# Lots of the two routers, place of the weight reads and of the residual reads in a fused two-layer kernel

## The chip, the cores and the metric

The kernel runs on one core of a Trainium2 chip. The metric is the device time of one execution in microseconds (us). Three executions of the kernel before are shown with their median, and one further execution was recorded by the hardware profiler. A core has five engines that run at the same time and wait for each other by semaphores: PE multiplies matrices, DVE, ACT and POOL work on tiles element by element, SP issues most of the DMA transfers. Each engine does its instructions in the order in which the program lists them.

## The reference, cut to what matters

There are 4096 tokens (64 sequences of 64) of 256 numbers. Four residual layers follow one another; the change lies in the last one, which has two mixtures of experts in a row, and in the end of the third, during which parts of the last are already worked.

```python
x = x + attn0(scan0(x, cond))
x = x + ffn0(cond2(x, cond))
x = x + mamba(rnn(x, cond))                    # x_mid: the kernel's name for this sum
x = x + ffn1(cond2_1(x, cond))

def cond2_1(x, t):                             # first mixture
    shared = sum(silu(x @ s_w1[e].T) * (x @ s_w3[e].T) @ s_w2[e].T for e in range(2)) / 2
    s = sigmoid(concat(x, t) @ W_router.T)     # 8 experts
    top = top_k(s + router_bias, 2)
    gates = s[top] / (sum(s[top]) + 1e-9)      # 0.5 each where the sum is not over 1e-9
    routed = sum(gates[e] * gelu(x @ r_w1[e].T) @ r_w2[e].T for e in top)
    return (shared + routed) / 4

def ffn1(x):                                   # second mixture
    score, top = top_k(x @ Wg.T, 2)            # 8 experts
    return sum(score[e] * (silu(x @ W1[e].T) * (x @ W2[e].T)) @ W3[e].T for e in top)
```

## The kernel before

Tokens are worked in 8 chunks of 512. Mamba (L684 to L952) takes 32 steps for each chunk: a step multiplies the input by B on POOL (hb, L864), exponentiates on ACT (dA, L871), scans on DVE (L903, two of them), multiplies by C on DVE (L905) and turns the product into a sum on PE (yp, L919). POOL's product is made two steps ahead. Between the steps a written-out order advances other work piece by piece: `urgent` and `pieces` are Mamba's own next parts (head, gates, finish, project), and `others` is the work beside it, at BESIDE (56) pieces for 32 steps. When `project` (L832) has written a chunk's x_mid (L846) it works off what is left of `others` and starts `beside` of the class Mixture (L1384) for that chunk. So the pieces of chunk c run during the period of chunk c + 1, and the last chunk's stay for later.

The pieces of a chunk are: the first router's scores, `choose` where a half of the tokens has its scores (L1401, after chunk 3: 16 tiles of 128 tokens at once), the `send` of a chunk of the first half (L1429), and `shared`, the shared expert of the chunk (L1446). `choose` makes the masks of the two best experts, counts with a scan and two products on PE how many tokens each expert has got so far, and from that the row of each token in a buffer in memory, in which every expert has a region (`Routing.choose`, L1045). `send` reads the chunk of x_mid, transposes it on PE (L1441), copies it into rows of 260 numbers on ACT (L1442), adds tags (L1436) and writes these with 8 indirect DMAs issued by POOL (L1100). Chunks 0 and 1 are sent during the periods of chunks 5 and 6 and chunks 2 and 3 during that of chunk 7. The pool of this work has one buffer of a kind.

After Mamba `mixtures` (L1541) runs. `rest` (L1484) reads the last chunk, makes its scores, chooses for the second half of the tokens (16 tiles), and sends chunks 4 to 7 while it works off the last chunk's shared expert: the up-products L1459, the product on POOL L1467, and the down-products L1475. `tiles` (L1123) makes a table of 39 tiles of 256 rows of the regions (L1131 to L1172). `Experts.run` (L1204) works them in order. `load` of a tile (L1209) reads two numbers of the table into registers of SP, asks for the weights of the tile's expert and then for its rows (`read`, L1105), which must wait until every send has landed. `turn` transposes the rows (L1224), `up` and `down` are the expert's products, and `give` (L1112) writes the result's rows by an indirect DMA of POOL. In the second experts (`Swiglu`) the up-products are L1335 and the weights of a tile (L1318 to L1323) have 2.16 MB.

Between the two lies the loop over chunks: `combine` (L1500) reads the shared expert's rows and the two experts' rows of each token (L1120) and adds them on DVE (L1507), and `Gate.chunk` (L1520) transposes the sum, makes the second router's scores, chooses for the chunk's 4 tiles and sends the chunk. At last a stage over the 8 chunks reads the second experts' rows and x_mid (L1563), adds them on PE (L1569) and DVE (L1578) and writes the output (L1579).

Memory on the core comes from pools that are opened and closed like a stack: in `mixtures` the pools of the first experts and of the loop (q1, q2, q3, qw) are closed before those of the second experts (g2, g3, gw) are opened in the same place. A tile that takes memory of a closed pool waits until the readers and writers of what lay there are done.

## Time and profile before

| what | us |
|---|---|
| three executions | 3247.75, 3249.04, 3253.38 |
| median of them | 3249.04 |
| the profiled execution, its own time | 3242.95 |
| its span, from the first to the last instruction | 3241.2 |
| Mamba's writes of x_mid (L846), from the span's start | 1106.5, 1260.6, 1405.6, 1548.6, 1716.1, 1870.0, 2019.7, 2133.7 |
| rest: its read of the last chunk; the last L1475 | 2150.5; 2228.4 |
| first experts: their last write of rows issued | 2424.9 |
| second router's sends: first and last issued | 2447.2; 2544.7 |
| second experts: first up-product; last write of rows issued | 2559.2; 3179.6 |

A profile of this kind gives the busy time of each engine, over the span or over a window of it. The lines in tenths cut the span in 40 slices of 81 us, with 9 for 90% or more. A group of instructions is shown with its line, its engine and the tiles that it writes and reads. The view of waits says for how long a line's instruction stood idle and what ended that. The chain of waits is followed back from the last instruction, at each step to what released it. The mean TensorE clock granted over the span was 0.894 of full speed.

### The profile page before, as it was taken

The numbers are of one execution on the slowest core, as the hardware profiler recorded it, in microseconds if no ns is written. First come the engines' busy times: TensorE is split into PE (matmuls) and PEld (weight loads), VectorE is DVE, ScalarE is ACT, GpSimd is POOL, SyncE is SP. The second block draws the span as 40 slices with busy tenths as digits, with TensorE's granted clock in tenths as the row PEclk, the third lists the DMA queues.
The fourth block names the chain that finished last, engine by engine and source line by source line (L and its number), as shares of the span: only waits on it lengthen the run. The fifth ranks groups of instructions, "written<-read, shape, count | busy, mean of one in ns | idle before, by whom it ended". The sixth has DMA issues, their size and how long they took to land. (4 is left out here: it accounts for less than half of the span.)

```text
span 3241.2 us, 38871 instructions
## 1 busy us (share of the span) xinstructions
PE 2586.4 (80%) x13918; PEld 1807.0 (56%) x13932; DVE 1757.8 (54%) x2860; ACT 1421.5 (44%) x2380; POOL 1308.3 (40%) x1091
## 2 busy tenths in 40 slices
PE   1978886777957788888778888677984599999995
PEld 1534443445734455555455555555761388888885
DVE  0166556884049988898978797731335322222221
ACT  0444443775456575766566666522331112222220
POOL 0011213542046766767577777824445311111110
PEclk9889997878967899999889899898996799999997
DMA  9598000000111212121122122224765655555545
GB/s 220 185 374 331 2 2 0 17 20 30 40 40 64 80 63 75 56 81 69 56 69 82 62 89 73 85 71 134 234 201 186 205 172 168 170 175 169 167 137 195
DMA packets 246305, 376.59 MB, mean 116 GB/s; under 512 B 45712, under 2 KB 147152, under 8 KB 245856
## 3 DMA queue, kind: packets, MB, share of 16 engines
q1 hardware_dynamic: 232480, 336.60, 32.1%
q0 software_dynamic: 13632, 37.50, 3.1%
q8 instruction: 110, 1.80, 0.2%
q14 instruction: 83, 0.68, 0.1%
HBM read 250.81 MB, written 123.22 MB: 115 GB/s over the span
## 5 line engine op out<-in xcount | busy, mean ns | idle before, releaser
L864 POOL TENSOR_TENSOR hb<-dx,Bn 128x1024 f32<-128x1024 f32 x256 | 601.1, 2358 | 267.2 <-PE yp L919 257.1
L903 DVE TENSOR_TENSOR_SCAN hb<-dA,hb 128x512 f32<-128x512 f32 x512 | 603.5, 1210 | 50.1 <-ACT dA L871 47.5
L871 ACT ACTIVATE dA<-delta,A 128x504 f32<-128x504 f32 x512 | 344.1, 683 | 293.4 <-DVE hb L903 290.7
L919 PEld LDWEIGHTS yp<-ident,hb 128*128 128x128 f32 x2048 | 270.1, 153 | 167.5 <-issue 128.1
L1335 PE MATMUL ps<-gxT,w 128*128 128x256 f32 x1560 | 360.3, 387 | 0.8 <-DVE gxT L1226 0.8
L905 DVE TENSOR_TENSOR hb<-hb,cb 128x1024 f32<-128x1024 f32 x256 | 312.3, 1220 | 78.6 <-PE cb L818 60.9
L1335 PEld LDWEIGHTS ps<-gxT,w 128*128 128x128 f32 x1560 | 292.7, 191 | 63.0 <-issue 25.2
L1459 PE MATMUL mq<-x,moe_s 128*128 128x256 f32 x896 | 258.5, 423 | 59.0 <-ACT up L1466 44.3
L919 PE MATMUL yp<-ident,hb 128*128 128x128 f32 x2048 | 304.4, 293 | 1.0 <-ACT yT L931 1.0
L1112 POOL DMA_INDIRECT ffn_y<-gy,to x78 | 74.8, 959 | 563.8 <-ACT gy L1248 559.4
L1339 DVE TENSOR_TENSOR gh<-gs,ps 128x256 f32<-128x256 f32 x195 | 81.2, 417 | 322.0 <-ACT gs L1338 321.1
L1459 PEld LDWEIGHTS mq<-x,moe_s 128*128 128x128 f32 x896 | 176.1, 212 | 121.1 <-ACT up L1466 51.4
L1247 PE MATMUL acc<-w,gh 128*128 128x256 f32 x936 | 230.1, 388 | 0.6 <-ACT gy L1248 0.6
L354 POOL TENSOR_TENSOR E<-E,z 128x1024 f32<-128x1024 f32 x32 | 60.8, 1900 | 417.3 <-DMA moe_x<-fill 204.8
L1248 ACT ACTIVATE gy<-acc,wt 128x256 f32<-128x256 f32 x156 | 73.9, 473 | 341.9 <-PE acc L1247 341.9
L1247 PEld LDWEIGHTS acc<-w,gh 128*128 128x128 f32 x936 | 168.4, 189 | 44.7 <-issue 25.5
L818 PE MATMUL cb<-parts,pick 80*128 80x512 bf16 x256 | 106.7, 417 | 94.7 <-DVE hb L905 79.5
L1338 ACT ACTIVATE gs<-ps 128x256 f32<-128x256 f32 x195 | 74.7, 383 | 231.7 <-PE ps L1335 226.3
L1236 DVE TENSOR_TENSOR to<-at,pick 128x2 int32<-128x2 f32 x78 | 12.6, 161 | 219.5 <-DMA ffn_y<-gy,to 125.5
L1112 POOL DMA_INDIRECT moe_y<-gy,to x78 | 74.8, 959 | 123.4 <-ACT gy L1248 121.0
L372 PE MATMUL acc<-oT,Wout 128*128 128x512 f32 x256 | 114.9, 608 | 9.3 <-ACT oT L366 9.3
L1475 PE MATMUL mq<-moe_s,sh 128*128 128x256 f32 x448 | 116.3, 398 | 4.8 <-ACT up L1466 4.8
(387 smaller groups left out, 4661.6 us busy)
## 6 DMA issues: line engine op xcount, KB each, us to landing
w<-in_ffn_W_dram SPq DMA_DIRECT2D x117, 640.0 KB, 4.6
Bn<-B SPq DMA_DIRECT2D x128, 512.0 KB, 3.6
moe_x<-fill SPq DMA_DIRECT2D x129, 260.0 KB, 5.0
ffn_x<-fill SPq DMA_DIRECT2D x129, 260.0 KB, 6.2
r<-in_moe_r_dram SPq DMA_DIRECT2D x78, 256.0 KB, 3.3
gx<-moe_x SPq DMA_DIRECT2D x39, 260.0 KB, 3.5
gx<-ffn_x SPq DMA_DIRECT2D x39, 260.0 KB, 4.1
x<-x_mid SPq DMA_DIRECT2D x16, 512.0 KB, 5.0
```

The source lines that it names most:

```text
L372: nc.tensor.matmul(ps, wa.Wout[:, o, ts(k, P)], v.o[:, o], start=(o == 0), stop=(o == H // 2 - 1))
L818: nc.tensor.matmul(t, pick[:, n : n + 1].to_broadcast([rows, P]), v.parts, start=True, stop=True)
L864: nc.gpsimd.tensor_mul(hb, vs[c].dx[p], Bn[:, n % NB, :].unsqueeze(1).to_broadcast([P, PI, CH]))
L871: nc.scalar.activation(decays[s][i][:, :, 1:], seq(vs[c].delta[p][:, i, :])[:, :, 1:], AF.Exp, scale=w.A[:, p * PI + i, n : n + 1],)
L903: ins = nc.vector.tensor_tensor_scan(h, dA[i].rearrange("p b l -> p (b l)"), h, 0.0, ALU.mult, ALU.add)
L905: ins = nc.vector.tensor_tensor(hb, hb, cb.unsqueeze(1).to_broadcast([P, PI, CH]), ALU.mult)
L919: nc.tensor.matmul(yp[i][:, t, :], hb[:, i, ts(t, P)], g.ident, start=(n == 0 and t == 0), stop=(n == S - 1 and t == CH // P - 1), is_tran ...
L1112: i = self.g.nc.gpsimd.indirect_dma_start(out=self.y, out_offset=bass.IndirectOffsetOnAxis(ap=to, axis=0), in_=y, in_offset=None)
L1247: nc.tensor.matmul(po[:, s, :], h, w, start=(i == 0), stop=(i == len(parts) - 1))
L1335: nc.tensor.matmul(ps[:, j, :], v.w12[:, k, ts(j * full + i, P)], v.xT[:, k, :], start=(k == 0), stop=(k == KD - 1))
L1459: nc.tensor.matmul(ps[:, i % 2, :], w[:, k, ts(i, P)], xu[:, k, :], start=(k == 0), stop=(k == KD - 1))
L1475: nc.tensor.matmul(ps[:, t, :], h[:, i, ts(t, P)], self.s2[:, i, :], start=(i == 0), stop=(i == NS - 1))
```

## The change

- BESIDE_LAST: during the last chunk's period 80 pieces of the other work are advanced in 32 steps instead of 56.
- `Routing` takes several sizes of a lot, with a `goes_on` tile for each.
- First router: `choose` runs after chunk 3 for chunks 0 to 3, after chunk 6 for chunks 4 to 6 and in `rest` for chunk 7. Two chunks are sent in each of the periods of chunks 5, 6 and 7; `rest` sends chunks 6 and 7, with 8 other pieces after each piece of a send. `rest` has a pool of its own.
- `Experts.run` asks for the weights of tiles 0 and 1 ahead of the rows of tile 0, and calls a hook after the reads of tile 1's rows have been issued.
- Second router: scores are kept for two chunks, `lot` chooses for both (8 tiles), and the tags are made in a tile of their own and copied by ACT. Some copies go from DVE to ACT.
- Pools: gw (the second experts' weights and rows) is opened ahead of the first experts' pools; the loop's rows have a pool of 5 buffers (qr).
- The residual: all 8 chunks of x_mid have tiles of their own (x3) and their reads stand in the hook.

```diff
     BESIDE = 56
+    BESIDE_LAST = 80
...
-            for _ in range((j + 1) * BESIDE // STEPS - j * BESIDE // STEPS):
+            most = BESIDE if c + 1 < NCH else BESIDE_LAST
+            for _ in range((j + 1) * most // STEPS - j * most // STEPS):
                 next(others, None)
...
-    def __init__(self, g, pool, x, name, most):
+    def __init__(self, g, pool, x, name, lots):
...
-        self.goes_on = pool.tile([P, NE, most], F32, name="goes_on")
-        nc.gpsimd.memset(self.goes_on, 1.0)
-        nc.gpsimd.memset(self.goes_on[:, :, 0:1], 0.0)
+        self.goes_on = {}
+        for n in lots:
+            t = self.goes_on[n] = pool.tile([P, NE, n], F32, name=f"goes_on{n}")
+            nc.gpsimd.memset(t, 1.0)
+            nc.gpsimd.memset(t[:, :, 0:1], 0.0)
...
-        n = self.most
+        n = sel.shape[1]
...
-        nc.vector.tensor_tensor_scan(flat(upto), flat(self.goes_on), flat(mine), 0.0, ALU.mult, ALU.add)
+        nc.vector.tensor_tensor_scan(flat(upto), flat(self.goes_on[n]), flat(mine), 0.0, ALU.mult, ALU.add)
...
-    def run(self, tables):
+    def run(self, tables, then=lambda: None):
+
         g, nc = self.g, self.g.nc
         S = TR // P
         table, rank = tables
+        SP = mybir.EngineType.SP
+
         def load(i):
-            v = SimpleNamespace()
-            SP = mybir.EngineType.SP
-            e = in_order(g.tc, table[0:1, 0, i : i + 1], [SP], NE - 1)
-            row = in_order(g.tc, table[0:1, 1, i : i + 1], [SP], NE * REG)
-            self.weights(v, e)
+            v = SimpleNamespace(i=i, rank=rank[:, i : i + 1])
+            self.weights(v, in_order(g.tc, table[0:1, 0, i : i + 1], [SP], NE - 1))
+            return v
+
+        def load_rows(v):
+            row = in_order(g.tc, table[0:1, 1, v.i : v.i + 1], [SP], NE * REG)
             v.x = self.pw.tile([P, S, RW], F32, name="gx")
             self.routing.read(v.x, row)
-            v.i, v.rank = i, rank[:, i : i + 1]
-            return v
         def turn(v):
             ps = bank(g, (P, KD, TR))
...
                 nc.scalar.mul(y[:, s, :], po[:, s, :], v.wt[:, s : s + 1])
                 self.routing.give(v.to[:, s : s + 1], y[:, s, :])
-        now = load(0)
+
+        now, after = load(0), load(1)
+        load_rows(now)
         turn(now)
-        after = load(1)
+        load_rows(after)
+        then()
         for i in range(NTL):
             self.up(now)
             if i + 1 < NTL:
                 turn(after)
-            nxt = load(i + 2) if i + 2 < NTL else None
+            nxt = None
+            if i + 2 < NTL:
+                nxt = load(i + 2)
+                load_rows(nxt)
             down(now)
             now, after = after, nxt
...
 
-    HALF = NCH // 2
+    LOTS = {NCH // 2 - 1: NCH // 2, NCH - 2: NCH // 2 - 1, NCH - 1: 1}
+
+    SENDS = {NCH // 2 + i: (2 * i, 2 * i + 1) for i in range(NCH // 2 - 1)}
     def __init__(self, g, pool, x):
         nc, a = g.nc, g.a
         self.g = g
-        self.routing = Routing(g, pool, x, "moe", NTT // 2)
+        self.routing = Routing(g, pool, x, "moe", [TT * n for n in self.LOTS.values()])
...
         pt = scores(g, work, self.Wr[:, :KD, :], x, self.cond[:, ts(c, CB)])
         g.nc.scalar.copy(self.score[:, ts(c, TT), :], pt)
         yield
-        if (c + 1) % self.HALF == 0:
-            self.choose(c // self.HALF, work)
+        if c in self.LOTS:
+            self.choose(c, work)
             yield
-        if c >= self.HALF:
-            yield from self.send(c - self.HALF, work)
-            if c == NCH - 2:
-                yield from self.send(c - self.HALF + 1, work)
+        for i in self.SENDS.get(c, ()):
+            yield from self.send(i, work)
         yield from self.shared(c, x, work)
-    def choose(self, half, work):
+    def choose(self, c, work):
+
         nc = self.g.nc
-        n = NTT // 2
-        t0 = half * n
+        n = TT * self.LOTS[c]
+        t0 = (c + 1) * TT - n
         s = work.tile([P, n, NE], F32, name="score")
         nc.scalar.activation(s, self.score[:, t0 : t0 + n, :], AF.Sigmoid)
         sel = work.tile([P, n, NE], F32, name="gsel")
...
         g.nc.sync.dma_start(x, g.x[:, :, (NCH - 1) * CH :])
         pt = scores(g, work, self.Wr[:, :KD, :], x, self.cond[:, (NCH - 1) * CB :])
         g.nc.scalar.copy(self.score[:, (NCH - 1) * TT :, :], pt)
-        self.choose(1, work)
+        self.choose(NCH - 1, work)
         others = self.shared(NCH - 1, x, work)
-        for c in range(self.HALF, NCH):
+        for c in range(2 * len(self.SENDS), NCH):
             for _ in self.send(c, work):
-                for _ in range(4):
+                for _ in range(8):
                     next(others, None)
         for _ in others:
             pass
...
         self.g = g
         self.Wg = pool.tile([P, KD, NE], F32, name="Wg")
         nc.sync.dma_start(self.Wg, g.a["ffn1_WgT"].rearrange("(k p) n -> p k n", p=P))
-        self.routing = Routing(g, pool, x, "ffn1", TT)
+        self.routing = Routing(g, pool, x, "ffn1", [self.LOT * TT])
+        self.score = pool.tile([P, NTT, NE], F32, name="gscore")
+        self.rows = {}
+
+    LOT = 2
     def chunk(self, c, rows, work):
         g, nc = self.g, self.g.nc
...
                 nc.tensor.transpose(ps[:, ts(t, P)], rows[:, t, ts(k, P)], g.ident)
             nc.scalar.copy(x[:, k, :], ps)
         pt = scores(g, work, self.Wg, x)
-        s = work.tile([P, TT, NE], F32, name="score")
-        sel = work.tile([P, TT, NE], F32, name="gsel")
-        nc.vector.tensor_copy(s, pt)
-        nc.vector.tensor_copy(sel, s)
-        masks = self.routing.choose(c * TT, sel, rows[:, :, D:], work)
+        nc.scalar.copy(self.score[:, ts(c, TT), :], pt)
+        self.rows[c] = rows
+        if (c + 1) % self.LOT == 0:
+            self.lot(c // self.LOT, work)
+
+    def lot(self, i, work):
+        nc = self.g.nc
+        n = self.LOT * TT
+        s = self.score[:, ts(i, n), :]
+        sel = work.tile([P, n, NE], F32, name="gsel")
+        nc.scalar.copy(sel, s)
+        tags = work.tile([P, n, RW - D], F32, name="gtags")
+        masks = self.routing.choose(i * n, sel, tags, work)
         for j in range(2):
-            mine = work.tile([P, TT, NE], F32, name="mine")
+            mine = work.tile([P, n, NE], F32, name="mine")
             nc.vector.tensor_mul(mine, s, masks[j])
-            nc.vector.tensor_reduce(rows[:, :, WT + j], mine, AX.X, ALU.add)
-        self.routing.send(c, rows)
+            nc.vector.tensor_reduce(tags[:, :, WT - D + j], mine, AX.X, ALU.add)
+        for c in range(i * self.LOT, (i + 1) * self.LOT):
+            rows = self.rows.pop(c)
+            nc.scalar.copy(rows[:, :, D:], tags[:, ts(c % self.LOT, TT), :])
+            self.routing.send(c, rows)
 
 def mixtures(g, mix, x, out):
...
         pool = lambda name, bufs: ctx.enter_context(tc.tile_pool(name=name, bufs=bufs))
         p1 = pool("e1", 1)
         gate = Gate(g, p1, x)
+        pw = pool("gw", 3)
         with ExitStack() as first:
             pool1 = lambda name, bufs: first.enter_context(tc.tile_pool(name=name, bufs=bufs))
-            q1, q2, q3, qw = pool1("q1", 1), pool1("q2", 2), pool1("q3", 3), pool1("qw", 3)
-            mix.rest(q2)
+            q1, qw = pool1("q1", 1), pool1("qw", 3)
+            with tc.tile_pool(name="rest", bufs=2) as work:
+                mix.rest(work)
+            q2, q3, qr = pool1("q2", 2), pool1("q3", 3), pool1("qr", 2 * gate.LOT + 1)
             Gelu(g, mix.routing, (q2, q3, qw)).run(mix.routing.tiles(q1))
             for c in range(NCH):
-                rows = q3.tile([P, TT, RW], F32, name="x2")
+                rows = qr.tile([P, TT, RW], F32, name="x2")
                 mix.combine(c, rows[:, :, :D], q3)
                 gate.chunk(c, rows, q2)
-        p2, p3, pw = pool("g2", 2), pool("g3", 3), pool("gw", 3)
-        Swiglu(g, gate.routing, (p2, p3, pw)).run(gate.routing.tiles(p1))
+        p2, p3 = pool("g2", 2), pool("g3", 3)
+        px = pool("gx", 1)
+        xs = []
+
+        def residual_chunks():
+            for c in range(NCH):
+                x = px.tile([P, KD, CH], F32, name=f"x3_{c}")
+                nc.sync.dma_start(x, g.x[:, :, ts(c, CH)])
+                xs.append(x)
+
+        Swiglu(g, gate.routing, (p2, p3, pw)).run(gate.routing.tiles(p1), residual_chunks)
         for c in range(NCH):
             rows = p3.tile([P, TT, 2, D], F32, name="rows3")
             gate.routing.fetch(c, rows)
-            x = p3.tile([P, KD, CH], F32, name="x3")
-            nc.sync.dma_start(x, g.x[:, :, ts(c, CH)])
+            x = xs[c]
             for k in range(KD):
                 po = bank(g, tag="acc")
```

More of the change, by code (lines that the diff above doesn't have):

```diff
@@ L1009 @@
 class Routing:
-    def __init__(self, g, pool, x, name, most):
+    def __init__(self, g, pool, x, name, lots):
         nc = g.nc
-        self.g, self.x, self.name, self.most = g, x, name, most
+        self.g, self.x, self.name = g, x, name
         self.sent, self.made = [], []
```

## The prediction

> **What bounds the kernel now.** I read the page first. No engine is full over the whole span, so an average decides nothing; each stage has to be read by itself.
>
> ```profile
> PE 2586.4 (80%) x13918; PEld 1807.0 (56%) x13932; DVE 1757.8 (54%) x2860; ACT 1421.5 (44%) x2380; POOL 1308.3 (40%) x1091
> PE   1978886777957788888778888677984599999995
> DVE  0166556884049988898978797731335322222221
> ```
>
> Next, the busy times by window, cut where Mamba writes a chunk of x_mid (L846 in the view by line). Columns: us, then busy PE, PEld, DVE, ACT, POOL, clock, DMA share, GB/s.
>
> ```profile
> 1260.60:1405.60 145.00, 121.63 (x569) 83.09 (x569) 127.23 (x122) 99.80 (x136) 103.93 (x50) 0.95 0.19 70
> 1548.60:1716.10 167.50, 133.71 (x570) 88.98 (x570) 138.51 (x154) 99.87 (x137) 104.82 (x55) 0.86 0.18 60
> 1716.10:1870.00 153.90, 127.77 (x576) 87.09 (x576) 128.25 (x124) 99.91 (x138) 112.09 (x59) 0.92 0.22 76
> 2019.70:2133.70 114.00, 85.70 (x420) 62.60 (x420) 82.56 (x76) 55.20 (x79) 72.70 (x48) 0.88 0.20 68
> ```
>
> The Mamba period is nearly full on DVE (127 of 145) and PE (122), so work put beside it isn't free: the period with the router's choice (second line) takes 20.1 us more than the mean of the three before it (154.1, 145.0, 143.0: 147.4), though DVE gained only some 10. The third line holds one chunk's sends. The last holds two chunks' sends, and there ACT's waits show:
>
> ```profile
> ACT rows L1442 <- DMA moe_x<-rows,row: 11.3, 1, 11.3
> PE mq L1441 <- ACT rows L1442: 9.5, 1, 9.5
> ```
>
> The second chunk's copy waits until the first chunk's eight sends have landed (the rows buffer is single there). PE and the scans stand behind it: the step at this place takes 14.6 us, its neighbours 3.6.
>
> At the second experts' start the DMA engines are the bound (first line: 2540 to 2580 us), then PE until 3175. In the final stage (3180 to 3240) it is DMA again, and the chain that ends the run shows it:
>
> ```profile
> DMA packets 8099, 10.50 MB, mean 263 GB/s; under 512 B 2614, under 2 KB 5494, under 8 KB 8096
> ```
>
> ```profile
> 3210.49 5.63 DMA x<-x_mid
> ...
> 3217.96 5.37 DMA x<-x_mid
> ...
> 3225.16 4.97 DMA x<-x_mid
> ...
> 3231.97 4.60 DMA x<-x_mid
> ```
>
> **What the Trainium skill says.** "DMA: Bandwidth & Descriptors", section "Anatomy of one DMA — SWDGE (gpsimd) path": a DMA issued by GpSimd has about 2.0 us of fixed cost, most of it the receipt of the write, before its semaphore fires. The trace agrees: sends land 2.4 us (least) and 2.5 us (median) after issue, so whoever reuses a sent buffer waits that after the eighth issue. Same page, "Issuing engines are not separate DMA queues": all DMAs end on the same 16 engines. That fits 2550 to 2575 us, where the engines are 0.95 busy at 303 GB/s: a transfer put ahead delays what stands behind it by its bytes. "ScalarE: Activation LUTs", section "What ACT_TABLE_LOAD costs": 1.283 us for a load; the trace has 1.28 at L808 and L871.
>
> **The change part by part.** Where buffers decide an order I read it from the order of the instructions on each engine of the changed kernel.
>
> *Second sends in two Mamba periods.* The periods of chunks 5 and 6 now hold two sends instead of one. Each second send has the single buffer's wait: 11.0 us (14.6 - 3.6). Low end 0 (the lone send of 1728 to 1738 us shows no stall: steps of 4.8, 4.0, 4.8, 4.0); high end 15, if the scans' inputs on POOL, at most three steps ahead, also run dry behind 8 x 1.265 us of sends. I take 11: 2 x 11.0 = +22.
>
> *Choice for 12 tiles of tokens inside the last period*, queued on DVE between scans. The choice for 16 cost 20.1; by size 15. The low end is its DVE work alone, 8.5 us in the tail for 16, so 6.4; the high end 20, as it consists of dependent small operations whose number doesn't shrink. I take +15.
>
> *80 pieces instead of 56.* The shared expert's second half ends inside the period. On PE 16 down-products now stand in one block in mid-period (7.2 us as in the tail, some +6.5 after what overlaps), and 16 near the last yp (+6.3, inside the tail's figure below). The second silu with its two table loads, formerly in the tail, lies between two decays: +4.2 from the 7.8 us step that held the first (7.8 - 3.6). The tail: last L905 at 2118.87 to rest's x load at 2150.51 is 31.6; it becomes 15.0 (last scan to x_mid's write, 14.8) + 6.3 = 21.3, so -10.3. Low end for the three together -10.3, high end +5; sum +0.4.
>
> Mamba up to rest: 22 + 15 + 0.4 = +37.
>
> *rest.* Two chunks' sends are left instead of four, 16 x 1.265 = 20.2 us of POOL less. The end is set by the shared expert, whose POOL products (L1467) stood behind sends: its two blocks of L1475 took 11.3 and 16.2 us where one without waits takes 7.2, so 4.1 and 9.0 were lost. In the new order each block's four products have eight sends ahead of or among them; with half the sends I take the longer loss as gone and the shorter as left. -9 (from -4 to -13).
>
> *First experts' start.* Two more weight reads of 0.26 MB stand before tile 0's rows on SP: 2 x 0.37 us issue plus transfer, +1.3. Low end 0.
>
> *Second router.* Before: first send at 2447.21, last at 2544.67, 64 x 1.265 = 81 us plus gaps of 16.5. Now the first choice needs two chunks' scores (second chunk's adds end at 2436.0, third's at 2441.1, and one more chunk's adds stand inside the choice), and takes 8 tiles per operation (0.26 us each, between 0.225 at 4 and 0.325 at 16): first send 9.1 later. Then gaps: the sixth buffer's reader waits for chunk 1's sends, so POOL idles some 10 us between the first lots, little later: 93.5 to the end of the last send instead of 98.4. Sum +4.2. From -8 (no idle) to +10.
>
> *Weights asked early.* In the changed order on SP they are not early: four x reads (2.10 MB) come first, the first of these reuses memory of the last chunks' rows and so waits for their sends, and the table of tiles (6.2 us of DVE) waits for the same sends; then follow tile 0's weights, tile 1's weights (2.16 MB) and only then tile 0's rows. Ahead of these rows stand 2.10 + 2.16 = 4.26 MB more than before, at 0.303 MB/us 14.1 us. Before, from the end of the last send (2545.63) to the end of the first up-products (2571.7) was 26.1, with 11.9 for these products, starved of weights; now the weights are there, so they take about 10. 14.1 - 1.9 - 1 (table and x reads overlap) = +11.3. Low end -7 (what the name promises), high end +16. The later four x reads (7 us) hide behind two tiles of 15.9 us of PE work; uncovered they cost 7.
>
> *Final stage.* Three of eight x reads were early already (2535.13). Five leave it: 5 x 0.524 = 2.62 MB at 0.292 MB/us (3200 to 3225 us) = -9.0. High end -5, low end -20.6, the sum of the four waits above, if these were latency and not rate; next late are the rows<-ffn_y reads, on the same engines.
>
> *At nothing:* the copies of scores, choices' inputs and tags that go from DVE to ACT (ACT is busy for 11.6 of the 98 us from 2447 to 2545; 1 to 3 us in all if uncovered), the extra goes_on memsets on POOL at the start (under 1 us), and the residual stage's larger buffers.
>
> Sum: 37 - 9 + 1.3 + 4.2 + 11.3 - 9 = +36. The profiled execution took 3242.95 us (span 3241.2 and 1.75 around it), so 3279 for a like one; the median of the runs shown is 6.1 higher, 3249.04, and 36 on it gives 3285.
>
> **Rivals.** (a) *The work beside Mamba is hidden.* For it: the lone send without a stall, 18 us of DVE idle in a period. Then the second sends and the choice cost nothing, and the tail gains 10.3: with -9 + 1.3 + 4.2 + 11.3 - 9 = -1.2 the sum is -11: 3238, faster. It decides where Mamba's part falls below +1.2. Against it: 20.1 for the choice and 11.3 for the double send, both measured beside Mamba.
> (b) *The stalls overlap.* While ACT waits for landing, hb inputs are made up, and the choice fills idle DVE: sends 6 each, choice 6.4, Mamba +19 instead of +37: sum +18, 3267.
> (c) *The change does what it says at the second experts:* weights -7 instead of +11.3, lots -8 instead of +4.2: 30.5 less, sum +6, 3255. Against it: the order on SP and the tile table's wait.
> (d) *Everything at its high end in Mamba* (15 each, 20, +5): 55, sum +54, 3303.
>
> **How the numbers follow.** Forecast as summed (3275 to 3298) 0.52; (b) 0.20 (3258 to 3275); (d) 0.09 (3298 to 3312); (c) 0.05; (a) 0.14. The range 3254 to 3308 leaves out (a) and a part of (c) and (d), under 2 in 10. A measurement of this kernel can tell about 0.2% (6.5 us) from no change. Faster: (a)'s larger part, 0.13; within: the rest of (a) and half of (c), 0.04; slower 0.83.
>
> **What would show it.** Right: L1442's wait of about 11 us on moe_x in the periods of chunks 5 and 6 too; a last period of some 140 us instead of 114; rest some 9 us shorter; the first up-products (L1335, then L1347) ending 37 us after the last send instead of 26; no wait on x in the final stage, which is 9 shorter. Wrong: Mamba periods of unchanged length (then (a)), weights landing before the last send (then (c)).

## The result, and the profile after

The changed kernel takes 3263.71 us (median of 6 executions, 3260.42 to 3266.59), the kernel before 3248.82 in the same session (6, 3247.74 to 3253.42). The ratio is 1.0042 with a 95% interval of 1.0029 to 1.0054: 0.4% slower. The forecast was 3285, with 3254 to 3308 as its range: the side was right, the size was not. Some 15 us were lost where 36 were forecast.

The profiled execution after has a span of 3262.3 us. I cut both spans at the same events. The first column is the kernel before, the second the changed one.

| stage | before, us | after, us | difference | forecast |
|---|---|---|---|---|
| up to Mamba's first write of x_mid | 1106.5 | 1111.9 | +5.4 | 0 |
| from there to rest's read of the last chunk | 1044.0 | 1052.2 | +8.2 | +37 |
| to the first experts' first result issued | 100.5 | 95.7 | -4.8 | -9 +1.3 |
| first experts, first to last result issued | 173.9 | 173.5 | -0.4 | 0 |
| to the second router's first send | 22.3 | 29.7 | +7.4 | +9.1 |
| its sends, first to last issued | 97.5 | 91.4 | -6.1 | -4.9 |
| to the second experts' first up-product | 14.5 | 30.5 | +16.0 | +11.3 |
| up-products to the last result issued | 624.1 | 624.2 | +0.1 | 0 |
| to the end | 58.0 | 53.2 | -4.8 | -9 |

The first line says nothing of the change: the kernels with the changed kernel's code up to there gave 1103.5 to 1113.5 in their profiles. Without it the trace shows +15.7; the ratio stands for 9 to 18 us. (The table ahead of the prediction gives 3179.6 for the second experts' last result issued; that is the last but one, and the last is at 3183.2.)

The windows view of the changed kernel, cut at its writes of x_mid (now L847), for the periods of chunks 5, 6 and 7; columns as before:

```profile
1721.50:1868.30 146.80, 120.51 (x570) 82.67 (x570) 128.07 (x122) 98.97 (x138) 119.71 (x68) 0.95 0.27 89
1868.30:2027.60 159.30, 129.74 (x600) 86.65 (x600) 126.33 (x121) 101.36 (x140) 119.65 (x67) 0.95 0.25 85
2027.60:2161.40 133.80, 100.24 (x470) 74.31 (x470) 93.16 (x108) 62.10 (x88) 79.16 (x79) 0.87 0.24 83
```

The period of chunk 5 is 7 us *shorter* than the 153.9 before, though a second send lies in it and POOL is 7.6 us busier. That of chunk 6 is 9.6 longer (149.7 before), the last one 19.9 longer. The waits for the rows buffer are there, though smaller than 11.3. The view of ACT's waits in the first and in the second of these windows:

```profile
ACT rows L1455 <- DMA moe_x<-rows,row: 4.4, 1, 4.4
```

```profile
ACT rows L1455 <- DMA moe_x<-rows,row: 7.3, 1, 7.3
```

So a wait that is plainly visible stands in a period that got shorter. That is the puzzle for the experiments.

At the second experts' start the view by line of the tile table's first step (L1136 before, now L1140) shows what holds it. First the kernel before, then the changed one:

```profile
L1136 DVE COPY n_e<-ps x1: 167/167/167, 2534.1 to 2534.1; 128x8 f32<-128x8 f32 x1
```

```profile
L1140 DVE COPY n_e<-ps x1: 165/165/165, 2557.2 to 2557.2; 128x8 f32<-128x8 f32 x1
...
  DMA ffn_x<-x,row: 25.8, 1
```

Before, the table was begun 10.6 us ahead of the last send (2544.7). In the changed kernel the last send is issued at 2554.4, and only when it has landed does the table begin, though it reads nothing that a send writes. Then the timeline of SP's queue, with start and length in us, first the kernel before:

```profile
2547.56 0.39 SPq L1318 DMA_DIRECT2D w<-in_ffn_W_dram  x1
```

```profile
2560.61 1.90 SPq L1595 DMA_DIRECT2D x<-x_mid  x4
2564.33 0.39 SPq L1330 DMA_DIRECT2D w<-in_ffn_W_dram  x1
...
2575.61 1.26 SPq L1111 DMA_DIRECT2D gx<-ffn_x  x2
```

The weights (2564.33) are asked for 9.9 us after the last send, where the kernel before did it after 2.9. The rows of tiles 0 and 1 follow 11.3 us later, behind both tiles' weights. (In the kernel's text the hook with the reads of x_mid stands behind those rows; on the queue four of these reads come first. The order on an engine has to be read from the engine.)

In the final stage no wait on x is left on the chain of waits; the reads of the experts' rows have taken its place:

```profile
3211.64 5.44 DMA rows<-ffn_y
...
3224.65 6.75 DMA rows<-ffn_y
```

### The profile page after: what moved, and what is told of

The parts are those of the page before. It is cut to its first block, busy times and chain, and to the rows that moved or that the text cites. A ratio compares the mean times of both kernels' runs of the same rounds, so it can differ in the third digit from the quotient of the medians.

```text
span 3262.3 us, 38769 instructions
## 1 busy us (share of the span) xinstructions
PE 2588.9 (79%) x13926; PEld 1804.4 (55%) x13926; DVE 1747.8 (54%) x2772; ACT 1431.6 (44%) x2406; POOL 1308.5 (40%) x1092
## 5 line engine op out<-in xcount | busy, mean ns | idle before, releaser
L872 ACT ACTIVATE dA<-delta,A 128x504 f32<-128x504 f32 x512 | 343.9, 683 | 276.4 <-DVE hb L904 271.9
L906 DVE TENSOR_TENSOR hb<-hb,cb 128x1024 f32<-128x1024 f32 x256 | 312.1, 1219 | 88.0 <-PE cb L819 68.7
```

The source lines that it names most:

```text
L872: nc.scalar.activation(decays[s][i][:, :, 1:], seq(vs[c].delta[p][:, i, :])[:, :, 1:], AF.Exp, scale=w.A[:, p * PI + i, n : n + 1],)
L906: ins = nc.vector.tensor_tensor(hb, hb, cb.unsqueeze(1).to_broadcast([P, PI, CH]), ALU.mult)
```

## The experiments

Each experiment was timed beside the kernel before on the same chip; the ratios are to it, with their 95% intervals. The names of periods are those of the chunk that Mamba works. "e1" stands for a label that begins with it. The ratios of e13 and e16 rest on 5 and 4 executions, those of the other experiments on 9 or more.

| kernel | ratio to before | interval |
|---|---|---|
| changed kernel | 1.0042 | 1.0029 to 1.0054 |
| e1 first mixture as before | 1.0002 | 0.9991 to 1.0014 |
| e2 first mixture alone | 1.0015 | 1.0006 to 1.0024 |
| b1 rest pool alone | 0.9994 | 0.9985 to 1.0003 |
| b2 rest pool, gw first | 1.0002 | 0.9994 to 1.0010 |
| e13 sends in pairs | 0.9956 | 0.9941 to 0.9970 |
| e15 empty pieces | 0.9972 | 0.9962 to 0.9982 |
| e14 two rows buffers | 1.0032 | 1.0022 to 1.0041 |
| e12 choice moved, sends as before | 1.0013 | 1.0005 to 1.0020 |
| e18 choice moved, pairs | 0.9973 | 0.9963 to 0.9983 |
| e17 56 pieces | 1.0020 | 1.0013 to 1.0027 |
| e5 second router, lot of one | 1.0038 | 1.0022 to 1.0054 |
| e3 residual reads at tile 4 | 1.0038 | 1.0028 to 1.0048 |
| e4 rows before tile 1's weights | 1.0014 | 1.0006 to 1.0023 |
| e8 table early | 0.9980 | 0.9971 to 0.9989 |
| e16 pairs and table early | 0.9876 | 0.9858 to 0.9893 |

The traces of these kernels, by stage, in us, from one profiled execution each. "Rest" is from rest's read of the last chunk to the first experts' first result, "start" from the second router's last send to the first up-product.

| kernel | period 5 | period 6 | period 7 | last write to read | rest | start | end |
|---|---|---|---|---|---|---|---|
| before | 153.9 | 149.7 | 113.9 | 16.9 | 100.5 | 14.5 | 58.0 |
| changed | 146.8 | 159.3 | 133.8 | 2.8 | 95.7 | 30.5 | 53.2 |
| e1 | 153.8 | 151.4 | 113.5 | 2.7 | 107.3 | 27.6 | 51.7 |
| e2 | 148.3 | 159.8 | 133.7 | 2.8 | 94.5 | 17.0 | 57.0 |
| b1 | 150.6 | 150.8 | 112.4 | 16.9 | 102.0 | 15.1 | 57.0 |
| b2 | 153.9 | 149.7 | 113.9 | 2.8 | 107.5 | 21.4 | 56.9 |
| e13 | 148.2 | 156.1 | 105.0 | 2.7 | 99.6 | 28.1 | 48.2 |
| e15 | 144.5 | 153.0 | 114.5 | 2.8 | 107.0 | 27.9 | 49.9 |
| e14 | 152.0 | 156.6 | 130.4 | 2.9 | 96.2 | 27.9 | 51.4 |
| e12 | 153.9 | 149.7 | 128.2 | 2.7 | 100.3 | 28.2 | 49.1 |
| e18 | 148.3 | 156.1 | 115.6 | 2.8 | 98.9 | 27.4 | 53.0 |
| e17 | 148.3 | 156.0 | 125.0 | 2.8 | 102.8 | 27.5 | 53.2 |
| e5 | 148.2 | 159.9 | 133.8 | 2.8 | 98.1 | 27.4 | 46.2 |
| e3 | 148.2 | 159.9 | 133.8 | 2.7 | 96.7 | 27.6 | 52.7 |
| e4 | 148.2 | 159.8 | 133.8 | 2.8 | 94.2 | 21.6 | 52.4 |
| e8 | 148.2 | 159.9 | 133.8 | 2.8 | 98.1 | 7.7 | 51.0 |
| e16 | 148.3 | 156.1 | 104.9 | 2.7 | 99.4 | 7.8 | 48.9 |

Two things limit what may be read from this table. Kernels in which Mamba's work has the same order don't agree exactly: before, e1, b1 and b2 have 150.6 to 153.9 in period 5, 149.7 to 151.4 in period 6 and 112.4 to 113.9 in period 7. So a difference of some 3 us in one period, from one profile each, proves little. And the clock granted to PE isn't the same in these windows (share of full speed, from the view of windows):

| kernel | period 5 | period 6 | period 7 |
|---|---|---|---|
| before | 0.92 | 0.94 | 0.88 |
| changed | 0.95 | 0.95 | 0.87 |
| e1 | 0.92 | 0.93 | 0.89 |
| b1 | 0.93 | 0.94 | 0.91 |
| e13 | 0.94 | 0.92 | 1.00 |
| e15 | 0.95 | 0.94 | 0.90 |
| e14 | 0.93 | 0.91 | 0.87 |
| e18 | 0.94 | 0.93 | 0.93 |
| e17 | 0.94 | 0.93 | 0.86 |

No experiment holds the clock fixed. What a move of work costs below is its cost with the clock that went with it.

### Which half of the change costs: e1 and e2

In e1 the changed kernel has the first mixture's order of before:

```diff
-    BESIDE_LAST = 80
+    BESIDE_LAST = 56
...
-    LOTS = {NCH // 2 - 1: NCH // 2, NCH - 2: NCH // 2 - 1, NCH - 1: 1}
+    LOTS = {NCH // 2 - 1: NCH // 2, NCH - 1: NCH // 2}
...
-    SENDS = {NCH // 2 + i: (2 * i, 2 * i + 1) for i in range(NCH // 2 - 1)}
+    SENDS = {4: (0,), 5: (1,), 6: (2, 3)}
...
-        for c in range(2 * len(self.SENDS), NCH):
+        for c in range(4, NCH):
...
-                for _ in range(8):
+                for _ in range(4):
```

> The changed kernel with the first mixture's order as before: 56 pieces, choice for 16 tiles twice, one send in the periods of chunks 5 and 6, four sends in rest. The traces put the whole part at +3.4 us (8.2 from the first write of x_mid to rest's read of the last chunk, -4.8 from there to the first experts' first result). Theory 1, the traces: about 3260. Theory 2, the prediction's sum (+37 - 9 + 1.3 = +29): 3234.

e2 is the other half: the kernel before with the changed LOTS, SENDS, BESIDE_LAST and rest's own pool, but with LOT = 1, the old place of gw and of the residual's reads, and tile 0's rows asked for ahead of tile 1's weights.

> The kernel before with the changed order of the first mixture alone (80 pieces, lots of four, three and one chunk, sends in pairs, rest with its own pool). Theory 1, the traces: 3249 + 3.4, about 3252. Theory 2, the prediction's sum: 3278.

e2 costs 0.15% (about 5 us) where the prediction's sum would be 29: the prediction's price of this half is refuted, the traces' +3.4 holds. e1 came out at 1.0002, some 13 us below the changed kernel and not the 4 that were expected. Its trace tells why: the last chunk's read comes 2.7 us after the last write of x_mid, as in the changed kernel, instead of 16.9. In e1 a part of the change that shortens the tail was still there. The two halves aren't additive, as both shorten the same tail.

### What shortens the tail: b1 and b2

b1 is the kernel before with `with tc.tile_pool(name="rest", bufs=2) as work: mix.rest(work)` in the place of `mix.rest(q2)` (qw is opened ahead of this pool, q2 and q3 behind it); all other work is ordered as before (some small copies of the second router are on ACT, as in e2). b2 adds one more:

```diff
         gate = Gate(g, p1, x)
+        pw = pool("gw", 3)
...
-        p2, p3, pw = pool("g2", 2), pool("g3", 3), pool("gw", 3)
+        p2, p3 = pool("g2", 2), pool("g3", 3)
```

> The kernel before with nothing changed but a pool of its own for rest, so that the last chunk's read needn't wait for memory of the work beside Mamba (16.9 us after the last write of x_mid before, 2.7 after). Theory 1: 14.2 less up to the read, of which the shared expert's leftover pieces ahead on PE give back some 7: 6 to 8 us less in all, ratio 0.998. Theory 2: the leftover pieces give back all of it: ratio 1.000.

> The kernel before with rest's own pool, as in b1, and the pool of the second experts' weights (gw) opened ahead of the first experts' pools, which puts rest's memory at 143.6 thousand, clear of the work beside Mamba; in b1 it was at 85.2 thousand and rest's read still waited 16.9 us. Theory 1: the place of gw is what shortens the tail: 2.7 instead of 16.9 there, the first experts 6 to 8 us earlier. Theory 2: something else in e1 did it: 16.9 again. The ratio itself also takes in what the second experts' start loses or gains by gw's place.

b1 changes nothing at this place: 16.9 still. In b2 it is 2.8, and from the first write of x_mid to the first experts' first result it takes 1137.4 us instead of 1144.5: 7.1 less. SP's queue shows what the read waits for, first in the kernel before, then in b2:

```profile
2133.65 0.37 SPq L846 DMA_DIRECT2D x_mid<-x  x1
...
2147.83 0.36 SPq L1481 DMA_DIRECT2D shared_rows<-up  x1
...
2150.51 0.46 SPq L1488 DMA_DIRECT2D xlast<-x_mid  x1
```

```profile
2134.60 0.36 SPq L847 DMA_DIRECT2D x_mid<-x  x1
2137.36 0.36 SPq L1502 DMA_DIRECT2D xlast<-x_mid  x1
```

Before, the read is issued 2.7 us behind the write of the last leftover piece's rows (L1481), 14 us after that of x_mid; in b2 it doesn't wait for these rows. With rest's own pool the place of gw makes the difference (moving gw without that pool was not tried): it moves rest's memory out of that of the work beside Mamba. The expectation for b1 was wrong. There is a second way to the same end: e2 has gw at its old place and yet 2.8, for in its order no piece is left. In b1 and b2 PE still works 48 of the shared expert's products after the last write of x_mid, in e2 none. The changed kernel has both, and either would do.

But b2 as a whole is at 1.0002, since the second experts start 6.9 us later. The same line of the tile table shows why, in b2's view by line:

```profile
L1140 DVE COPY n_e<-ps x1: 166/166/166, 2540.8 to 2540.8; 128x8 f32<-128x8 f32 x1
...
  DMA ffn_x<-x,row: 12.5, 1
```

Pushed up by gw's 57 KB a partition, the loop's row buffers lie where the table's work tiles come later, and the table waits for the last sends (where the tiles lie is read from the kernel; the trace shows the wait). One line gives 7 us and takes 7.

### What a second send costs: e13, e15, e14

e13 is e1 with one line changed, so that no send is left in the last period:

```diff
-    SENDS = {4: (0,), 5: (1,), 6: (2, 3)}
+    SENDS = {4: (0, 1), 5: (2, 3)}
```

> The changed kernel with the choices and the 56 pieces as before and two sends in the periods of chunks 5 and 6, none in the last, four in rest. Theory 1, the traces: the two periods together 2 to 5 us longer than with one send each (153.8 + 151.4 in e1), and the last period shorter than 113.5 by what its two sends cost. Theory 2, the prediction: +22 for the two periods.

Periods 5 and 6 together take 304.3 us, with one send each 305.2 (e1): two more sends cost nothing there that stands out of the spread of 3 us, where the prediction had +22. And the last period loses 8.5, rest another 7.7: of the shared expert's leftover products 19 instead of 48 stand ahead of the last chunk's scores on PE, and these scores begin 3.8 us after the read instead of 11.5. The last period also has the full clock throughout, where the line of the kernel before in the prediction has 0.88:

```profile
2024.90:2129.90 105.00, 85.53 (x448) 63.71 (x449) 82.69 (x76) 57.01 (x80) 60.85 (x34) 1.00 0.19 61
```

How much of the 8.5 is the clock and how much the two sends is not separated. In all e13 gains 0.46% on e1 (0.9956 against 1.0002, about 15 us).

Why does the period of chunk 5 get shorter with more in it? e15 takes e1 and puts three pieces that do nothing where the second send's three would be:

```diff
         for i in self.SENDS.get(c, ()):
             yield from self.send(i, work)
+            if c < 6:
+                yield
+                yield
+                yield
```

> The kernel of e1 (first mixture's order as before, its own pool for rest) with three pieces that do nothing after the send in the periods of chunks 5 and 6: the shared expert's pieces come three pieces later, as they do behind a second send, but no second send is there. With one send the periods were 153.8 and 151.4, with two 148.2 and 156 to 160. Theory 1: the place of the shared expert's pieces (its silu and table loads against Mamba's own) makes the difference: chunk 5's period goes to 148 or below. Theory 2: the place doesn't matter: 153.8 and 151.4 again.

Period 5 falls from 153.8 to 144.5 with no work taken away, and the kernel as a whole is 0.3% faster than e1. So the place of the shared expert's pieces decides: 9.3 us in this period against e1 (6 to 9 against the kernels of e1's order), and +1.6 in the next. The steps of Mamba, from one product with C (L906) to the next, put 3.2 of these 9.3 at the first silu of the shared expert, 3.7 at a single later step, and 2.4 at the period's end. The timeline of ACT shows what happens at the silu. First e1, then e15, each around the shared expert's silu and Mamba's own (L752):

```profile
1750.49 1.28 ACT L1483 ACT_TABLE_LOAD   x1
1751.78 1.91 ACT L1483 ACTIVATE sh<-sh 128x2048 f32<-128x2048 f32 x1
...
1754.26 0.57 ACT L1479 COPY up<-mq 128x512 f32<-128x512 f32 x1
1754.85 1.28 ACT L872 ACT_TABLE_LOAD   x1
1756.15 1.29 ACT L872 ACTIVATE dA<-delta,A 128x504 f32<-128x504 f32 x2
1757.60 1.28 ACT L752 ACT_TABLE_LOAD   x1 [0.16 <-DVE xc L748]
1758.89 1.91 ACT L752 ACTIVATE xc<-xc 128x2048 f32<-128x2048 f32 x1
...
1761.78 1.28 ACT L872 ACT_TABLE_LOAD   x1
```

```profile
1759.26 1.28 ACT L1487 ACT_TABLE_LOAD   x1
1760.55 1.91 ACT L1487 ACTIVATE sh<-sh 128x2048 f32<-128x2048 f32 x1
1762.37 1.89 ACT L752 ACTIVATE xc<-xc 128x2048 f32<-128x2048 f32 x1
...
1764.84 1.28 ACT L872 ACT_TABLE_LOAD   x1
```

In e1 the two silus are 7 us apart with a decay (L872, an exp) between them: four table loads. Three pieces later they stand side by side: two loads. The Trainium skill, "ScalarE: Activation LUTs", section "What ACT_TABLE_LOAD costs", gives about 2.66 us for each switch to a different set, the load and a drain. This trace shows half of it: from the end of the copy at 1754.83 to the start of the exp at 1756.15 lie 1.3 us, the load (1.28) and almost nothing else. So two loads fewer are an estimated 2.6 of the 3.2 us of these steps, worked out from the 1.3 of the trace.

The loads don't explain the whole. Over period 5 e1 has 13 of them, e13 and e15 have 12, since at the second silu e15 has one more; and in period 6, where e15 is only 1.6 us longer, it has 14 against 11.

The single step of 3.7 us is another matter. No table is loaded in it. PE works the same eight down-products of the shared expert ahead of the product that the step waits for (cb), first e1, then e15:

```profile
1791.12 3.78 PE L1488 MATMUL mq<-moe_s,sh 128*128 128x256 f32 x8
1794.70 0.63 PE L819 MATMUL cb<-parts,pick 80*128 80x512 bf16 x1
1795.37 1.22 DVE L906 TENSOR_TENSOR hb<-hb,cb 128x1024 f32<-128x1024 f32 x1 [4.38 <-PE cb L819]
```

```profile
1790.21 1.99 PE L1492 MATMUL mq<-moe_s,sh 128*128 128x256 f32 x8
1792.04 0.38 PE L819 MATMUL cb<-parts,pick 80*128 80x512 bf16 x1
1792.46 1.22 DVE L906 TENSOR_TENSOR hb<-hb,cb 128x1024 f32<-128x1024 f32 x1 [0.60 <-PE cb L819]
```

The granted clock is 0.50 in e1 from 1785.5 to 1795.5 and 1.00 in e15 from 1782 to 1802. The step takes 7.8 us with the one and 4.1 with the other. Why the other place of the pieces went with another clock is not shown, nor are the last 2.4 us taken apart.

Against e15, where the pieces stand three later but no second send is made, e13's periods are 148.2 - 144.5 = 3.7 and 156.1 - 153.0 = 3.1 us longer. That is about the spread between profiles, so the size is rough; it is a third of the 11.0 that the prediction put down for each.

e14 takes away what makes the second send wait, with a second buffer:

```diff
-        rows = work.tile([P, TT, RW], F32, name="rows")
+        rows = work.tile([P, TT, RW], F32, name=f"rows{c % 2}")
```

> The changed kernel with two buffers for the rows of a send beside Mamba, so that the second send of a pair needn't wait for the first one's landing. ACT's waits there were 4.4, 7.3 and 5.9 us in the three periods. Theory 1, the prediction's: these waits are on the path; the three periods (146.8 to 148.2, 159.3 to 159.9, 133.8) lose up to 17 us together. Theory 2: the steps catch up later, where DVE and PE have room, and the three together change by less than 5.

Of 17.6 us of waits for landed sends (4.4, 7.3 and 5.9) 1.8 are left. The three periods take 439.0 together, the changed kernel's 439.9 (441.9 in e3, e5 and e8, which have the same Mamba): 1 to 3 us less. Theory 2 holds by its number. Its reason, that later steps catch up, is not shown. In period 5 the two steps at the wait do get shorter (6.8 and 7.1 become 4.8 and 4.0), but others get longer (4.2 two steps later becomes 7.0, and 5.1 near the end 8.4), and the clock is lower in periods 5 and 6 than in the changed kernel (0.93 and 0.91 against 0.95 and 0.95). So the wait alone doesn't set the length of the period; a lower clock may have taken back what two buffers gave.

### The last period: e12, e18, e17

e12 is the changed kernel with SENDS = {4: (0,), 5: (1,), 6: (2, 3)} and four sends in rest, four pieces after each of their steps.

> The changed kernel with the sends as before (one in the periods of chunks 5 and 6, two in the last, four in rest), so that of the first mixture's order only the lots of four, three and one chunk and the 80 pieces are changed. The last period was 113.5 with the order as before (e1) and 133.8 with all changes. Theory 1: the choice for 12 tiles and the pieces that came from the tail make nearly all of the 20: 130 to 134. Theory 2, the prediction's sizes: 113.9 + 15 + 10.7 + 6.3 = 146.

128.2 is 14.7 above e1: theory 1, slightly below its range. e18 is e13 with the changed LOTS, so that the choice for chunks 4 to 6 alone is moved; e17 the changed kernel with BESIDE_LAST = 56.

> The kernel of e13 (56 pieces, pairs of sends in the periods of chunks 5 and 6, four sends in rest) with the choice for chunks 4 to 6 in the last period. There e13 has 105.0, and 99.6 from rest's read to the first experts' first result. Theory 1, the prediction's size: +15 in the period, 3 to 5 back in rest, +10 to +12 in all. Theory 2: the choice fills idle DVE (its own work is 6.4): +6 in the period, 3 to 5 back, +1 to +3. Theory 3: the choice is hidden and rest gains: below 0.

> The changed kernel with 56 pieces in the last period instead of 80. Theory 1: the 80 pieces only move work from the tail into the period: the last period gets shorter than 133.8 and the time from the last write of x_mid to the first experts longer by as much, the sum (133.8 + 2.7 + 95.7 = 232) within 3 us. Theory 2: denser pieces cost scans: the sum falls by 5 or more. Theory 3, the prediction's: pieces after the period cost 10 more: the sum rises by 10.

The last period can now be built up: 105.0 without choice and sends (e13); 115.6 with the choice (e18, +10.6); 125.0 with chunks 4 and 5 sent in it as well (e17, +9.4); 133.8 with 80 pieces (+8.8). The clock of these four is 1.00, 0.93, 0.86 and 0.87, so each price but the last includes a lower clock than that of the kernel before it in the row. The choice gives back only 0.7 in rest, so its +10.6 lies between theories 1 and 2, nearer to the first; the ratios, 0.9956 and 0.9973, put it at some 5 to 6 us, with intervals that overlap. The 80 pieces give back 7.1 in rest: in the sum as I had written it, from period 7 on, they cost 1.7, which is theory 1. But period 6, which the expectation had left out, ends with a write of x_mid in the denser steps and is 3.3 longer: +5 in all, and 1.0020 against 1.0042 agrees with it. That the denser steps make these 3.3 is not tested; e12, with 80 pieces and one send a period, has 149.7 there. None of these moves gains anything that the simple pairs of e13 don't.

### The second router's lots: e5

e5 has LOT = 1 in the changed kernel.

> The changed kernel with the second router choosing for one chunk at a time. Theory 1, the traces (119.8 us from the first experts' last result to the last send before, 121.1 after): the lots of two cost 1.3, so 3262. Theory 2, the prediction's +4.2: 3259.5. Theory 3: the lots gain, as fewer operations on DVE are needed: 3268 or more.

From the first experts' last result to the last send it takes 120.6 us with one chunk in a lot and 121.1 with two: the first send comes 5.9 earlier, the sends take 5.4 longer. Lots of two move the time, they don't save it. The ratio (1.0038, 1.0022 to 1.0054) can't tell the two apart from each other; the trace does.

### The second experts' start: e3, e4, e8

In e3 the residual's reads get a dependence on tile 4's transposed rows, and so stand behind those of the first tiles in SP's order.

```diff
...
-        then()
         for i in range(NTL):
+            if i == 4:
+                then(now.turned)
...
+                tc.add_manual_dep(ins.ins, turned.ins.name, info, reason="after this tile")
```

> The changed kernel with the eight early reads of x_mid issued only when tile 4 of the second experts has been turned; the two tiles' weights still ahead of tile 0's rows. Theory 1: the 2.10 MB of four reads ahead of the weights cost 7 us at the start of the second experts: 3257. Theory 2: these reads lie beside the making of the tile table, which the weights wait for anyway: 3262 to 3264.

The start is 27.6 us, exactly as in e1, which has these reads ahead of the weights (and 27.4 to 28.2 in seven further kernels with them; the changed kernel's own 30.5 is the highest). The 2.10 MB that I had priced at 7 us cost nothing: they run while the table is being made, as theory 2 had it. e4 asks for tile 0's rows ahead of tile 1's weights as well:

```diff
-        now, after = load(0), load(1)
+        now = load(0)
         load_rows(now)
         turn(now)
+        after = load(1)
         load_rows(after)
```

> The changed kernel with the early reads of x_mid moved to tile 4 and tile 0's rows asked for ahead of tile 1's weights, as before. With the reads at tile 4 alone the first up-product came 27.6 us after the last send. Theory 1: tile 1's 2.16 MB ahead of the rows cost 2.16 / 0.303 = 7 us: the up-product comes 20 to 21 us after the last send, about 7 us less time. Theory 2: tile 0's own weights are still missing when the rows are there, so nothing is gained: 27 us.

21.6: theory 1, 6.0 less. Of the 13 us that this stage is longer than before, 7 are left: the table, which begins only after the last landing. e8 tests that with one line moved:

```diff
+        tables = gate.routing.tiles(p1)
         p2, p3 = pool("g2", 2), pool("g3", 3)
         px = pool("gx", 1)
...
-        Swiglu(g, gate.routing, (p2, p3, pw)).run(gate.routing.tiles(p1), residual_chunks)
+        Swiglu(g, gate.routing, (p2, p3, pw)).run(tables, residual_chunks)
```

> The changed kernel with one line moved: the table of tiles is made before the pool of the eight residual tiles is opened, so its memory is no longer that of the last chunk's rows. Theory 1: the table and through it both tiles' weights wait for the last sends only because of that memory; now they are asked for while the sends run, and only tile 0's rows wait: the first up-product comes about 10 us after the last send instead of 27 to 30, 17 to 20 us less time, about 3245. Theory 2: the transfers hold each other up, and weights beside sends delay the sends by as much: within 5 us of the changed kernel.

The start falls to 7.7, half of what it was in the kernel before, and the ratio from 1.0042 to 0.9980. The table and SP's queue in e8 (the view by line and the timeline; the last send is at 2556.7):

```profile
L1140 DVE COPY n_e<-ps x1: 154/154/154, 2525.9 to 2525.9; 128x8 f32<-128x8 f32 x1
```

```profile
2532.63 0.39 SPq L1330 DMA_DIRECT2D w<-in_ffn_W_dram  x1
...
2540.61 2.34 SPq L1335 DMA_DIRECT2D w<-in_ffn_W_dram  x1
2559.46 1.27 SPq L1111 DMA_DIRECT2D gx<-ffn_x  x2
2560.90 4.86 SPq L1596 DMA_DIRECT2D x<-x_mid  x8
```

Both tiles' weights are asked for 16 to 24 us before the last send and only the rows wait for it. This is what the change says of itself; one overlap in memory had kept it from happening. (In e8 all eight reads of x_mid come behind the rows; by e3 their place costs nothing.) The sends took 92.3 us beside these transfers and 91.4 without: theory 2 is refuted.

### Both together: e16

> The kernel of e13 (choices and 56 pieces as before, sends in pairs in the periods of chunks 5 and 6) and the table made before the residual tiles' pool is opened, as in e8. If the two gains are independent (17 us of e13 against e1, 20 to 23 of the table): ratio to the kernel before 0.988 to 0.990, about 3210. If weights beside sends or the earlier end of Mamba take one of them back: 0.993 or more.

e16 is e13 with e8's line moved: 3208.86 us, ratio 0.9876 (0.9858 to 0.9893), 1.2% below the kernel before and 1.7% below the changed one. The two gains add up: the last period 104.9, the start 7.8.

## Why the prediction was wrong, point by point

**Second sends, +22: the step that failed.** "I take 11: 2 x 11.0" priced a second send by the length of one step of the last period. Measured, the two periods change by -1 when each gets its second send (e13 against e1; +2.5 between the kernel before and the changed one), and with the waits taken away the three periods lose 1 to 3 us of 439.9 (e14). Against a kernel with the pieces at the same place a second send costs about 3 (e13 against e15), and the place of the shared expert's pieces, which I didn't price at all, gave 9.3 in one period. The prediction had the lower bound in hand: it named the lone send of 1728 to 1738 us that shows no stall. It took the double send's 14.6 us step as loss without asking whether the period got longer by it. And the step isn't the send's alone: from 2036.5 to 2056.5 us the granted clock was 0.50, and eight up-products of the shared expert took 3.78 us in it that take 1.99 at 2074.5 us. The prediction's own lines show the clock of each window (0.95, 0.86, 0.92, 0.88), and it weighed it nowhere.

**Choice, +15:** right in kind, +10.6 by measure (e18). Scaling period 4's 20.1 by size was too much; that period also has the lowest clock of the four lines, 0.86.

**80 pieces and the tail.** I had +10.7 in the period and -10.3 for the tail. The tail was right in kind: from the last product with C to rest's read it takes 24.0 us instead of 31.6, so -7.6. The 6.3 more up to the write of x_mid came as forecast (21.2 instead of 14.8; e14, with 80 pieces as well, has 15.7, so the match is partly luck), and the wait behind leftover pieces is gone. That gw's place removes the same wait (b2) was not foreseen, and so in the changed kernel the 80 pieces were no longer needed for it: by themselves they cost 5 there (e17). One of the prices in the period was misread: the 7.8 us step does not hold the silu. It runs from 2078.9 to 2086.7, the silu's table loads are at 2068.8 and 2072.0, and the granted clock was 0.50 from 2080.5 to 2087.0. The last period is 19.9 longer, where my parts made 32 (15, 10.7 and 6.3).

**First mixture in all:** forecast 37 - 9 + 1.3 = +29, in the trace +8.2 - 4.8 - 0.4 = +3. These 26 us are more than the whole difference of 20 between forecast (36) and trace (15.7); later stages cost 6 more than forecast.

**rest, -9:** -4.8. The sum was made for the read as its start; the leftover pieces and the choice's smaller size were not seen apart.

**Second router, +4.2:** right in its parts (+7.4 for +9.1, -6.1 for -4.9), +1.3 in all.

**Weights not early, +11.3:** right in direction, and its size, +13 to +16, is near by luck. The 14.1 us of bytes were half wrong: the residual's reads cost 0 (e3), tile 1's weights 6.0 (e4). In place of the reads it is the table that costs: the prediction read in the order of instructions that it waits for the last sends, and then booked it as overlap ("- 1") instead of as a chain. (14.1 - 1.9 - 1 is 11.2, not 11.3.) That chain and the weights behind it are worth 20 to 23 us (e8).

**Final stage, -9:** -4.8 in the changed kernel, -4.8 to -11.8 in the kernels with these reads early. The four waits on x are gone as forecast; the reads of rows wait in their place.

**The rivals.** Rival (b), stalls that overlap, gave 3267, came nearest to the measured 3263.7 and had a chance of 0.20. Its mechanism is right in part: it put each second send at 6 and the choice at 6.4; measured are about 3 and 10.6. That its sum fits is partly luck, as it had +19 for Mamba where the trace has +8.2, and 6 less than measured for the later stages. No rival named the clock or the place of the pieces.

## What to carry to other kernels

A wait in the trace is not yet a cost: price an inserted piece by the length of periods with and without it. When pieces are interleaved by count, adding a piece shifts all later ones, and that alone was worth more here than the piece cost (9.3 us against about 3). Look at the granted clock of a window before giving its length to the work in it: one step took 7.8 us at 0.50 and 4.1 at 1.00. And when a pool is opened earlier or a tile kept longer, list what each later tile now overlies: here the same move gave 7 us and took 7, and one line's place decided over 20.

## What the runs showed that was not expected

Three empty pieces in two periods made a kernel 0.3% faster (e15 at 0.9972, e1 at 1.0002) without doing anything. The clock granted in the last period went from 0.88 to 1.00 with two sends moved out of it (e13, and e16 again), though PE is busy for the same 85 to 86 us there. And 4.3 MB of weights ran beside the indirect sends at almost no cost to these (92.3 us against 91.4, e8 against the changed kernel), where the DMA engines as a whole were 0.71 busy (2530 to 2560 us of e8).
